# The seam between two convolution layers: where the second silu tile lies, how long a scratch tile is, and when the last store is issued

## Chip, core and metric

The kernel runs on one core of a Trainium2 chip. The metric is the device time of one execution in microseconds; lower is better. The core has five engines with queues of their own: TensorE (PE), VectorE (DVE), ScalarE (ACT), GpSimd (POOL) and SyncE (SP, which issues most of the transfers). Sixteen DMA engines carry out all transfers.

## The reference

The input x is 4 images of 16 channels, 256 by 256, float32. There are two residual layers:

```python
x = x + _L0_conv_ref(_gn(x), conv_w, conv_b)       # layer 0
x = x + _L1_conv_ref(_gn(x), base_weight, ...)     # layer 1
```

`_gn` is a group norm over 8 groups of two channels. Layer 0 makes 25 logits per channel and pixel with a 3x3 convolution, takes their softmax and weighs the pixel's 5x5 neighbourhood with it. Layer 1 is a 3x3 convolution of 16 to 16 channels on two kinds of features of the normed x: silu, and eight cubic B-spline bases. Its own group norm needs the sums of layer 0's result over a whole image.

## The kernel before

**Layer 0** works on 64 strips (4 images, 2 halves of the height, 8 strips of 32 columns). For each strip TensorE makes logits, ScalarE the exponentials `e`, GpSimd the products with the neighbourhood (L860), VectorE the sums (L700) into `nd`. The division follows in three VectorE instructions (L720 to L722), and GpSimd subtracts the result from `xc`, the block of x of four strips, so that `xc` holds layer 0's result x1 (L728). When a block is complete, `statistics` takes its sums and `store` writes it to `x1s` in HBM (L781). Both are put off by some steps with `after(k, f)`, which runs `f` k steps later. ScalarE's queue issues the stores; the last one only, of the last block of image 3, is issued by GpSimd. The last block also has a form of its own of the statistics, `last_statistics`: sixteen short VectorE instructions on `xc` (L759 and L763), and then eight of GpSimd on 128x8 elements (L766 to L773).

**Layer 1** works on 64 units (16 for each image), each of 16 rows. A unit n loads three things from `x1s` through SyncE's queue:

- `load_x` (L942): two halves of 1 MB into one of three tiles `xta`, `xtb`, `xtc` (unit n takes tile n % 3), each channel repeated on eight partitions;
- `load_tiles` (L957): four pieces of 128 KB into the upper 64 partitions of one of three silu tiles `sl[n % 3]`;
- and later `store` (L1026) writes the two pieces of output.

`silu` (L972, ScalarE) makes the silu features in the lower 64 partitions of the same tile. `features` makes the splines in two halves: ScalarE takes the distances to the grid in place (L990), `minus_r` is VectorE's share (L158), and `spline` goes through ScalarE (L163 to L166) and VectorE (L167 to L169) with scratch tiles `ta` for the first half and `tb` for the second, into `ring`. TensorE multiplies `ring` (L1036) and the silu tile (L1046) by the weights. `sides` (L1071) clears the two border columns of a silu tile with GpSimd.

The order within each engine is written out: `in_order` ties the instructions of each engine one behind the other as they are in the program, and `marks` and `behind` let the beginning of layer 1 move between the last instructions of layer 0. Thus units 0 and 1 are loaded while layer 0 is ending.

The tiles of layer 1 lie in the memory that layer 0's tiles gave back. They are placed one behind the other in the order in which the pools are opened, and a tile that covers an address of an older tile waits for everything that still uses the older one:

```python
xt0, tmp0, tmp1 = fixed("xta", XT), temps("ta"), temps("tb")
xt1, pad = fixed("xtb", XT), fixed("pad", [P, W + 2])[0]
ring = fixed("ring", [P, 3 * RU + 2, W + 2])[0]
SL = [P, RU // RT, W + 2]
sl = fixed("sl", SL)
xtt = xt0 + xt1 + fixed("xtc", XT)
sl += fixed("slb", SL, 2)
```

So the order of places is xta, ta, tb, xtb, pad, ring, one silu tile, xtc, two silu tiles. The order of the first loads on SyncE's queue is x of unit 0, silu rows of unit 0, x of unit 1, then x of unit 2, silu rows of unit 1, x of unit 3, silu rows of unit 2 and so on.

Of the kernel before, what the change touches and what calls it, by code (L numbers as in the profile page):

```python
# [11 lines left out]
F32 = mybir.dt.float32  # L12
# [22 lines left out]
def conv_preact_kernel(  # L35
# [13 lines left out]
    B, C, H, W = x.shape  # L49
    G = 8  # L50
    GC = C // G
    P = 128
# [23 lines left out]
    RU = 16  # L76
# [47 lines left out]
    for r in range(RT):  # L124
        p = P // 2 + SROWS.index(r + 1) * C
# [278 lines left out]
    with tc.tile_pool(name="prep0", bufs=2) as prep, tc.tile_pool(  # L404
        name="pre", bufs=1
    ) as pre, tc.tile_pool(
        name="xin", bufs=3
    ) as xin, tc.tile_pool(name="stat", bufs=2) as stat, tc.tile_pool(
        name="pstat", bufs=1, space=PSUM
# [116 lines left out]
        for b in range(B):  # L526
            st = stat.tile([P, G, NH * (GC if b == 0 else 1), 6], F32, name=f"st0_{b}", tag=f"st0{min(b, 1)}")
            for hf in range(NH):
                n = b * NH + hf
                t = loaded.pop(0)  # L530
# [80 lines left out]
    def newest(engine):  # L611
        return [i for i in nc.cur_bb.bb.instructions if i.engine == engine][-1]
# [7 lines left out]
    def layer0(shift):  # L620

        arm = "g" if shift else ""
        marks = {}
        first = len(nc.cur_bb.bb.instructions)
        with tc.tile_pool(name=f"prep{arm}", bufs=2) as prep, tc.tile_pool(
            name=f"im{arm}", bufs=NIM
        ) as imp, tc.tile_pool(name=f"l0{arm}", bufs=2) as l0, tc.tile_pool(
            name=f"nd{arm}", bufs=3
        ) as ndp, tc.tile_pool(name=f"x1{arm}", bufs=3) as x1p, tc.tile_pool(name=f"ptr{arm}", bufs=1, space=PSUM) as ptr, tc.tile_pool(
            name=f"plog{arm}", bufs=3, space=PSUM  # L630
# [44 lines left out]
            def load_xc(n):  # L675
                b, hf, s = strips[n]
                xc = x1p.tile([P, C, CX], F32, name=f"xc_{n}{arm}", tag="xc")
                nc.sync.dma_start(
                    xc, x[b, :, hf * P : (hf + 1) * P, s * SW : s * SW + CX].rearrange(
                        "c p w -> p c w")  # L680
                )
                return xc
# [5 lines left out]
            def after(k, f, *args):  # L688

                later.append([k, partial(f, *args)])  # L690
# [34 lines left out]
            def apply(n, nd, xc):  # L725
                w0 = strips[n][2] * SW % CX
                v = xc[:, :, w0 : w0 + SW]
                nc.gpsimd.tensor_sub(v, v, nd[:, 1])  # L728
                seeds[1:] = [newest(POOLE)]
                if w0 + SW == CX:  # L730
                    if n == len(strips) - 1:
                        after(1, last_statistics, n, xc)
                    else:
                        for g in range(G):
                            after(1 + g, statistics, n, xc, g)
                    after(2, store, n, xc)

            def columns_of(n):
                b, hf, s = strips[n]
# [35 lines left out]
            def store(n, xc):  # L775
# [10 lines left out]
                    name=nc.get_next_instruction_name(), engine=mybir.EngineType.Activation,  # L786
# [8 lines left out]
            nxc, xc = load_xc(0), None  # L795
            ahead = iter(())
            for n, (b, hf, s) in enumerate(strips):
# [12 lines left out]
                if s * SW % CX == 0:  # L810
                    xc = nxc

                nd = ndp.tile([P, 2, C, SW], F32, name=f"nd_{n}{arm}", tag="nd")
                for j in range(0, SW, JG):
                    if j % CI == 0:
                        k = n * nci + j // CI
# [68 lines left out]
    def layer1(arm, last, marks, seeds):  # L885
# [5 lines left out]
        with ExitStack() as pools:  # L891
            def pool(name, bufs=1, **kw):
                return pools.enter_context(tc.tile_pool(name=f"{name}{arm}", bufs=bufs, **kw))


            def temps(name):
                p = pool(name)
                return [p.tile([P, RU // 2 + 1, W], F32, name=f"{name}{k}{arm}") for k in range(3)]

            def fixed(name, shape, n=1):  # L900
                p = pool(name)
                t = [p.tile(shape, F32, name=f"{name}{k}{arm}") for k in range(n)]
                return t

            XT = [P, RU + 1, W]
            xt0, tmp0, tmp1 = fixed("xta", XT), temps("ta"), temps("tb")
            xt1, pad = fixed("xtb", XT), fixed("pad", [P, W + 2])[0]
            ring = fixed("ring", [P, 3 * RU + 2, W + 2])[0]
            SL = [P, RU // RT, W + 2]
            sl = fixed("sl", SL)  # L910
            xtt = xt0 + xt1 + fixed("xtc", XT)
            sl += fixed("slb", SL, 2)
            yop = pool("yo", 3)
            pstat = pool("pstat1", space=PSUM)
            py = pool("py", 4, space=PSUM)
# [1 line left out]
            units = [(b, u) for b in range(B) for u in range(NU)]  # L917

            def rows(t, dims, r):

                return bass.AP(tensor=t.tensor, offset=t.offset + r * W, ap=dims)
# [4 lines left out]
            def halves(u):  # L926
                lo, hi = span(u)
                mid = (lo + hi + 1) // 2
                return lo, ((lo, mid), (mid, hi))
# [8 lines left out]
            def load_x(n, half):  # L938
                b, u = units[n]
                lo, hs = halves(u)  # L940
                a, z = hs[half]
                nc.sync.dma_start(  # L942
                    xtt[n % 3][:, a - lo : z - lo, :],
                    rows(x1s[b], [[CP, C], [0, NS], [1, (z - a) * W]], u * RU - 1 + a),
                )
# [3 lines left out]
            def load_tiles(n):  # L949
                b, u = units[n]  # L950
                t = sl[n % 3][P // 2 :, :, 1 : W + 1]
                for p, q in outside(u):
                    nc.gpsimd.memset(t[p : p + C, q], 0.0)  # L953
                for k, d in enumerate(SROWS):
                    q0 = 1 if (u, d) == (0, 0) else 0
                    q1 = RU // RT - (1 if (u, d) == (NU - 1, RD - 1) else 0)
                    nc.sync.dma_start(  # L957
                        t[k * C : (k + 1) * C, q0:q1, :],
                        rows(x1s[b], [[CP, C], [RT * W, q1 - q0], [1, W]], u * RU - 1 + d + q0 * RT),
                    )  # L960

            def outside(u):

                return [
                    (SROWS.index(d) * C, q)
                    for at, d, q in ((0, 0, 0), (NU - 1, RD - 1, RU // RT - 1)) if u == at
                ]

            def silu(n):
                b, u = units[n]  # L970
                t = sl[n % 3][0 : P // 2, :, 1 : W + 1]
                nc.scalar.activation(  # L972
                    t, sl[n % 3][P // 2 :, :, 1 : W + 1], AF.Silu,
                    scale=sc[b][0][P // 2 :], bias=sc[b][1][P // 2 :],
                )
                for p, q in outside(u):
                    nc.gpsimd.memset(t[p : p + C, q], 0.0)

            def features(n, between):
                b, u = units[n]  # L980
                lo, hs = halves(u)
                r0 = place(n)
                parts = [
                    (a, z, xtt[n % 3][:, a - lo : z - lo], [t[:, 0 : z - a, :] for t in tmp])
                    for (a, z), tmp in zip(hs, (tmp0, tmp1))
                ]

                def distance(a, z):
                    t = xtt[n % 3][:, a - lo : z - lo]
                    nc.scalar.activation(t, t, AF.Abs, scale=sc[b][2], bias=sc[b][3])  # L990


                if n > 0:
                    distance(lo, hs[1][1])
                    minus_r(parts[1][3][0], parts[1][2])
                for k, (a, z, xt, tmp) in enumerate(parts):
                    if n == 0:
                        distance(a, z)
                    if k == 1:
                        between()  # L1000
                    spline(ring[:, r0 + a : r0 + z, 1 : W + 1], xt, *tmp, given=n > 0 and k == 1)
# [20 lines left out]
            def store(lag=LAG1):  # L1022
                if len(waiting) >= lag:
                    b, u, yo = waiting.pop(0)
                    for g in range(2):
                        nc.sync.dma_start(  # L1026
                            rows(out[b], [[W, 8], [H * W, C], [1, W]], u * RU + 8 * g), yo[:, g]
                        )
# [31 lines left out]
            load_tiles(0)  # L1060
            for half in range(2):
                load_x(1, half)
            nc.gpsimd.tensor_copy(pad, edge[:, 4:5].to_broadcast([P, W + 2]))
            for e in (0, W + 1):
                nc.gpsimd.tensor_copy(
# [3 lines left out]
            def sides(t):  # L1069
                for e in (0, W + 1):  # L1070
                    nc.gpsimd.memset(t[:, :, e : e + 1], 0.0)  # L1071

            halo(0)
            set_up = newest(POOLE).name
            sides(sl[0])
            features(0, put)
            first_silu = len(nc.cur_bb.bb.instructions)
            silu(0)
            for n in range(len(units)):
                if n % 2:  # L1080
                    next(more, None)
                if n > 0:
                    features(n, put)
                    silu(n)
                    halo(n)
                if n + 2 < len(units):
                    for half in range(2):
                        load_x(n + 2, half)
                store()
                if n + 1 < len(units):  # L1090
                    load_tiles(n + 1)
                outputs(n)
                if n == 0:
                    for t in sl[1:]:
                        sides(t)
            for _ in range(LAG1):
                put(1)
                store(1)
# [15 lines left out]
    with tc.If(fast > 0) as small_logits:  # L1114
        layer1("", *layer0(False))
    with small_logits.Else():
        layer1("g", *layer0(True))
# [42 lines left out]
```

## Time and profile before

| | us |
|---|---|
| median of 3 runs | 3076.96 (3075.38 to 3077.81) |
| the profiled execution | 3072.98 |
| its span | 3070.8 |
| VectorE busy | 2959.4 (96%) |
| TensorE busy | 2807.1 (91%) |
| ScalarE busy | 2238.8 (73%) |
| GpSimd busy | 1954.8 (64%) |
| mean granted TensorE clock | 0.967 |

All durations come from the one profiled execution, whose span is 2.2 us shorter than its time. The two layers show in its busy shares over time: GpSimd is busy for nine tenths of layer 0 and for hardly any of layer 1, ScalarE is full in layer 1. Layer 0's last sums on VectorE end at about 2046 us; the stretch up to 2100 us is the seam. An engine's line in a timeline gives its start, its duration, the engine, the line of the kernel and the operation with the tiles that it writes and reads; brackets give the idle time before it and the instruction that ended it. "SPq" is SyncE issuing a transfer: its duration is that of the issue and not of the transfer.

### The profile page before, as it was taken

To read this page: it belongs to the slowest core of one execution; us is meant where nothing else is said; L and a number is where in the kernel's file an instruction comes from. 1 tells how busy PE (TensorE), PEld (TensorE's weight loads), DVE (VectorE), ACT (ScalarE), POOL (GpSimd) and SP (SyncE) were. 2 spreads that over 40 slices of the span, in tenths; PEclk is the share of its full clock that TensorE was granted. 3 is DMA by queue.
4 is the path that set the end of the run, shared out by engine and by line. 5 is a ranking of instruction groups with operands and counts; after the bars stand their busy time and mean duration, and the time that the engine had idled before them with its cause. 6 is when DMAs were issued, how large, how long until landed. Compare 5 with 4: busy or idle time off the path is not lost.

```text
span 3070.8 us, 39744 instructions
## 1 busy us (share of the span) xinstructions
PE 2807.1 (91%) x14248; PEld 1450.3 (47%) x14248; DVE 2959.4 (96%) x1587; ACT 2238.8 (73%) x2587; POOL 1954.8 (64%) x744
## 2 busy tenths in 40 slices
PE   4599999999999999999999999957999999999998
PEld 3366656656566656666666656531222222222222
DVE  7599999999999999999999999997999999999997
ACT  6466675576765666765645646667999999999996
POOL 4299999999999999999999999971100100000000
PEclk7699999999999999999999999978999999999999
DMA  8988977879888778878867657659999999999994
GB/s 272 297 222 224 247 218 197 232 184 256 225 218 233 201 206 238 234 209 226 224 162 189 184 149 199 175 118 179 193 193 196 199 195 188 198 197 201 189 199 90
DMA packets 350929, 626.29 MB, mean 204 GB/s; under 512 B 41330, under 2 KB 216676, under 8 KB 334852
## 3 DMA queue, kind: packets, MB, share of 16 engines
q1 hardware_dynamic: 318020, 605.29, 80.6%
q10 hardware_dynamic: 30960, 15.73, 1.8%
q0 software_dynamic: 1744, 2.64, 0.3%
q8 instruction: 117, 1.92, 0.3%
q14 instruction: 88, 0.72, 0.1%
HBM read 513.95 MB, written 104.24 MB: 201 GB/s over the span
## 4 chain that ended last, share of the span: by engine, by line
DVE 69%; issue 11%; PE 7%; DMA 6%; ACT 3%; POOL 2%; SPq 2%; DVEq 0%; ACTq 0%; POOLq 0%
DVE nd L700 44%; PE lg L832 4%; DVE ta L168 4%; DVE ta L167 4%; DVE tb L168 4%; DVE tb L167 4%; DVE tb L158 2%; POOL e L860 1%; DVE yo L1019 1%; DVE r L721 1%; PE lg L836 1%; DVE nd L720 1%; DMA xta<-x1s 1%; DVE nd L722 1%; DMA an<-hsl 1%
## 5 line engine op out<-in xcount | busy, mean ns | idle before, releaser
L860 POOL TENSOR_TENSOR e<-e,u 128x1600 f32<-128x1600 f32 x512 | 1789.4, 3552 | 48.4 <-ACT e L855 30.5
L832 PE MATMUL lg<-wm,am 128*128 128x400 f32 x4096 | 1737.1, 505 | 82.6 <-ACT e L855 47.3
L700 DVE TENSOR_REDUCE nd<-e 128x128 f32<-128x3200 f32 x512 | 1748.0, 3478 | 28.3 <-POOL e L860 28.1
L836 PE MATMUL lg<-wn,an 97*128 97x400 f32 x2048 | 1345.8, 657 | 15.3 <-DMA an<-hsl 15.2
L855 ACT ACTIVATE e<-lg 128x800 f32<-128x800 f32 x1024 | 820.5, 838 | 709.6 <-DVE nd L700 472.3
L832 PEld LDWEIGHTS lg<-wm,am 128*128 128x128 f32 x4096 | 761.8, 192 | 402.3 <-ACT e L855 96.4
L1036 PE MATMUL yp<-ring,wt 128*32 128x512 f32 x6144 | 748.7, 600 | 97.0 <-DVE ring L169 73.1
L836 PEld LDWEIGHTS lg<-wn,an 97*128 97x128 f32 x2048 | 388.3, 190 | 333.9 <-issue 23.1
L1036 PEld LDWEIGHTS yp<-ring,wt 128*32 128x32 f32 x6144 | 205.4, 109 | 632.3 <-issue 428.9
L953 POOL MEMSET sl<- 16x256 f32 x4 | 1.2, 306 | 307.6 <-PE yp L1046 301.4
L953 POOL MEMSET slb<- 16x256 f32 x4 | 1.2, 307 | 299.8 <-PE yp L1046 299.7
L168 DVE TENSOR_TENSOR ta<-ta,ta 128x2048 f32<-128x2048 f32 (+1 forms) x64 | 147.4, 2304 | 3.4 <-ACT ta L166 3.3
L169 DVE SCALAR_TENSOR_TENSOR ring<-ta,ta 128x2048 f32<-128x2048 f32 (+1 forms) x64 | 147.8, 2310 | 2.5
L747 ACT ACTIVATE z<-xc,nrm 128x256 f32<-128x256 f32 x240 | 144.2, 601 | 5.4 <-POOL xc L728 1.3
L169 DVE SCALAR_TENSOR_TENSOR ring<-tb,tb 128x2048 f32<-128x2048 f32 x64 | 145.6, 2275 | 2.5
L168 DVE TENSOR_TENSOR tb<-tb,tb 128x2048 f32<-128x2048 f32 x64 | 145.3, 2270 | 0.0
L1046 PE MATMUL yp<-slb,ws 64*32 64x512 f32 (+1 forms) x1008 | 128.2, 602 | 0.0
L166 ACT ACTIVATE ta<-ta 128x2048 f32<-128x2048 f32 (+1 forms) x64 | 123.4, 1928 | 2.0
L193 POOL TENSOR_TENSOR d<-d,nrz 128x8 f32<-128x8 f32 x4 | 2.7, 666 | 188.1 <-DVE d L191 188.1
L166 ACT ACTIVATE tb<-tb 128x2048 f32<-128x2048 f32 x64 | 120.5, 1883 | 0.0
L972 ACT ACTIVATE slb<-slb,q 64x2048 f32<-64x2048 f32 x42 | 87.9, 2094 | 21.5 <-DMA slb<-x1s 20.4
L728 POOL TENSOR_TENSOR xc<-xc,nd 128x512 f32<-128x512 f32 x64 | 83.3, 1302 | 8.3 <-DVE nd L722 8.3
(195 smaller groups left out, 2099.3 us busy)
## 6 DMA issues: line engine op xcount, KB each, us to landing
am<-hst SPq DMA_DIRECT2D x512, 194.6 KB
u<-hs SPq DMA_DIRECT2D x320, 288.0 KB
an<-hsl SPq DMA_DIRECT2D x512, 129.8 KB
xta<-x1s SPq DMA_DIRECT2D x40, 1024.0 KB
xtb<-x1s SPq DMA_DIRECT2D x40, 1024.0 KB
xtc<-x1s SPq DMA_DIRECT2D x40, 1024.0 KB
am<-hst SPq DMA_DIRECT2D x256, 129.8 KB
slb<-x1s SPq DMA_DIRECT2D x164, 128.0 KB
```

Of the source, the lines that this page charges most:

```text
L166: nc.scalar.activation(s1, r1, AF.Square, scale=2.0)
L167: nc.vector.scalar_tensor_tensor(s2, t, 2.0, s2, ALU.subtract, ALU.mult)
L168: nc.vector.tensor_mul(s1, s1, r1)
L169: nc.vector.scalar_tensor_tensor(f, s2, 0.0, s1, ALU.min, ALU.subtract if given else ALU.add)
L700: nc.vector.tensor_reduce(nd[:, :, :, j : j + JG].rearrange("p t c j -> p t j c"), e.rearrange("p t j m c d -> p t j c m d"), AX.XY, ALU.add,)
L747: nc.scalar.activation(z, v, f, scale=nrm[b][:, 0, g : g + 1], bias=nrm[b][:, 1, g : g + 1], accum_out=st1[b][:, t, g, columns_of(n) : col ...
L832: nc.tensor.matmul(lg[:, i, :NL], lhsT=am[:, o : o + P], rhs=wm.rearrange("p m c d -> p (m c d)"), start=True, stop=False,)
L836: nc.tensor.matmul(lg[:, i, :NL], lhsT=an[:, o : o + P], rhs=wn.rearrange("p m c d -> p (m c d)"), start=False, stop=True,)
L855: nc.scalar.activation(ev, lg[:, :, :NL], AF.Exp)
L860: nc.gpsimd.tensor_tensor(e[:, 1].rearrange("p j m c d -> p j (m c) d"), e[:, 0].rearrange("p j m c d -> p j (m c) d"), uv, ALU.mult,)
L1036: nc.tensor.matmul(yp[t * M : (t + 1) * M], lhsT=wt[:, d, e].rearrange("p r o -> p (r o)"), rhs=ring[:, r0 + t * RT + d : r0 + t * RT + d ...
L1046: nc.tensor.matmul(yp[t * M : (t + 1) * M], lhsT=ws[v, e].rearrange("p r o -> p (r o)"), rhs=sl[n % 3][v, t : t + NT + 1 : NT, e : e + W], ...
```

## The change

Three edits, all at the seam:

1. The second silu tile is placed beside the first, ahead of `xtc`; only the third stays behind `xtc`. Its rows (unit 1) are loaded directly behind the x of unit 1, ahead of the x of unit 2, and its borders are cleared together with those of the first.
2. The scratch tiles `tb` of the second half of a unit have 8 rows instead of 9.
3. The last store of x1 is issued directly behind the last subtraction, ahead of `last_statistics`; it was issued two steps after it, behind the statistics. All other stores stay where they were.

```diff
                 if w0 + SW == CX:
                     if n == len(strips) - 1:
+                        store(n, xc)
                         after(1, last_statistics, n, xc)
                     else:
                         for g in range(G):
                             after(1 + g, statistics, n, xc, g)
-                    after(2, store, n, xc)
+                        after(2, store, n, xc)
...
-            def temps(name):
+            def temps(name, rows):
                 p = pool(name)
-                return [p.tile([P, RU // 2 + 1, W], F32, name=f"{name}{k}{arm}") for k in range(3)]
+                return [p.tile([P, rows, W], F32, name=f"{name}{k}{arm}") for k in range(3)]
...
-            xt0, tmp0, tmp1 = fixed("xta", XT), temps("ta"), temps("tb")
+            xt0, tmp0, tmp1 = fixed("xta", XT), temps("ta", RU // 2 + 1), temps("tb", RU // 2)
...
-            sl = fixed("sl", SL)
+            sl = fixed("sl", SL, 2)
             xtt = xt0 + xt1 + fixed("xtc", XT)
-            sl += fixed("slb", SL, 2)
+            sl += fixed("slc", SL)
...
             for half in range(2):
                 load_x(1, half)
+            load_tiles(1)
...
             halo(0)
             set_up = newest(POOLE).name
-            sides(sl[0])
+            for t in sl[:2]:
+                sides(t)
...
                 store()
-                if n + 1 < len(units):
+                if 0 < n < len(units) - 1:
                     load_tiles(n + 1)
                 outputs(n)
                 if n == 0:
-                    for t in sl[1:]:
-                        sides(t)
+                    sides(sl[2])
```

In the profile before, the silu tiles are called `sl` (the first) and `slb` (the second and third); with the change they are `sl` (the first and second) and `slc` (the third).

## The prediction

> **What bounds the kernel now.** I read the two-stage balance first, then the seam between the stages. Over most of the span VectorE is the engine without pauses: the profile gives it 96%, and the chain of waits 69%. Only the seam can change here, so I read the timeline of each engine from 2046 to 2105 us. First VectorE: start, duration, operation, and in brackets the idle time before it and its releaser.
> ```profile
> 2079.96 2.29 DVE L169 SCALAR_TENSOR_TENSOR ring<-tb,tb 128x2048 f32<-128x2048 f32 x1
> 2098.99 1.23 DVE L158 TENSOR_SCALAR tb<-xtc 128x2048 f32<-128x2048 f32 x1 [16.74 <-ACT xtc L990]
> ```
> VectorE ends unit 1 at 2082.25 and stands still for 16.74 us. It waits for ScalarE's distances of unit 2 (L990), and ScalarE was itself held up one instruction earlier:
> ```profile
> 2072.56 1.91 ACT L166 ACTIVATE tb<-tb 128x2048 f32<-128x2048 f32 x1
> 2093.03 2.09 ACT L972 ACTIVATE slb<-slb,q 64x2048 f32<-64x2048 f32 x1 [18.57 <-DMA slb<-x1s]
> 2095.15 3.80 ACT L990 ACTIVATE xtc<-xtc,q 128x4096 f32<-128x4096 f32 x1
> ```
> The silu of unit 1 wants its rows. SyncE issues those at 2086.19, in its queue behind the load of xtc:
> ```profile
> 2063.87 1.16 SPq L942 DMA_DIRECT2D xtc<-x1s  x2
> 2086.19 1.73 SPq L957 DMA_DIRECT2D slb<-x1s  x4
> 2087.96 2.02 SPq L942 DMA_DIRECT2D xta<-x1s  x2
> ```
> SyncE's own waits give the reason: 21.1 us for `x1s<-xc`, the last store of layer 0, because slb lies where that store reads. GpSimd shows why the store is late:
> ```profile
> 2062.57 1.27 POOL L728 TENSOR_TENSOR xc<-xc,nd 128x512 f32<-128x512 f32 x1 [8.32 <-DVE nd L722]
> ...
> 2068.38 2.13 POOL L767 TENSOR_TENSOR sq<-sq,nrm 128x8 f32<-128x8 f32 x1
> 2070.47 0.20 POOL L768 TENSOR_TENSOR sq<-mv,nrm 128x8 f32<-128x8 f32 x1
> ...
> 2079.96 1.28 POOL L781 DMA_DIRECT2D x1s<-xc  x1
> 2086.19 0.22 POOL L1071 MEMSET slb<- 128x8 f32 x4 [4.95 <-DMA x1s<-xc]
> ```
> Its data is complete at 2063.84, but the eight small statistics (L766 to L773) stand ahead of it until 2080. So the path through the seam is: statistics, store, slb, silu, distances. The last question is what limits the time behind it. In the windows view (length, the engines' busy time, clock, DMA share, GB/s):
> ```profile
> 2060.50:2065.00 4.50, 3.05 (x16) 0.80 (x20) 3.25 (x7) 3.64 (x1) 1.51 (x2) 0.50 0.00 0
> 2065.00:2074.50 9.50, 9.50 (x82) 2.40 (x74) 9.02 (x17) 9.41 (x6) 7.05 (x6) 0.91 0.98 216
> 2076.50:2081.50 5.00, 2.27 (x14) 0.29 (x10) 4.96 (x3) 0.00 (x0) 4.65 (x3) 0.89 0.00 0
> 2087.00:2184.00 97.00, 78.82 (x642) 19.65 (x638) 82.47 (x46) 90.29 (x43) 5.78 (x4) 0.89 1.03 192
> ```
> Before 2087 the DMA engines have holes (shares of 0.00); from 2087 to 2184 they are full. At 2184 comes ScalarE's one later wait for data, 1.84 us for slb at 2186.38, and VectorE loses 1.45 us at 2198.03 from it. So for the first hundred microseconds of layer 1 the loads are as much the limit as VectorE.
>
> **What the Trainium skill says.** "DMA: Bandwidth & Descriptors", Issuing engines are not separate DMA queues: loads and stores of all issuers share the same 16 engines. The trace agrees: the share is 1.03 with all of them running. The same page, Queues, rings and completion order: on each engine a queue's descriptors are consumed in ring order. In half-microsecond windows slb's bytes run from 2087.0, end in a dip at 2091.2, and xta's follow until a dip at 2100.2; so 4.2 us for four slb pieces and 9.0 for two xt halves, one behind the other. "SBUF — State Buffer", Who interferes with whom: a two-input VectorE instruction blocks a GpSimd instruction that reads SBUF. The trace agrees: L767 takes 2.13 us beside two-input instructions and L768 0.20 us. That is what makes the statistics long.
>
> **The change part by part.** Times are those of the profiled execution.
>
> *Store behind the subtraction.* Nothing is added: the same DMA moves past L977 and L766 to L773. It follows L728 at about 2063.9. From issue to landing it took 6.2 us (DMA issues view), so it lands at 2070.1, 16 us earlier. Its 1.28 us of issue end at 2065.2; the statistics wait for VectorE until 2067.2 anyway, so they keep their times, and their first reader (scales of image 3) comes many units later. VectorE's bn_stats (L759) read the same xc while it is stored; two readers need no wait.
>
> *Second silu tile beside the first.* In the changed program's list of waits, the rows of unit 1 (now sl1) wait only for older loads, and stand directly behind xtb (2048.1). Issue ends by about 2053, since the third piece waits for the first piece of sl0, landed by 2052.5. In ring order their 4.2 us of bytes follow xtb's, which end at 2060.1, into the empty stretch 2060.5 to 2065. Two more memsets of 0.06 us stand ahead of L728, under its 8.32 us of waiting. Silu(1) then runs right behind L166, at 2074.5 to 2076.6 instead of 2093.03. Cost zero.
>
> *What is late next.* The list puts the store's wait at the load of xtc: it waits for the store, POOL, ACT, DVE. So it leaves at 2070.1 instead of 2063.87, 6.2 us later, and queued behind it on SyncE are xta of unit 3, slc of unit 2 and xtb of unit 4, none of which could go earlier than 2087 before. From xtc's issue to its first bytes 1.15 us (2063.87 to 2065.0), 9.5 us of bytes, and 1.25 us until ScalarE starts (xtb: 2060.1 to 2061.36): 11.9, so 2082.0. A thin tail of xtc's traffic until 2076.3 makes it 13.6 at most: 2083.7. L990 and the start of VectorE take 3.84: VectorE starts unit 2 at 2085.9 (to 2087.6) instead of 2098.99. **13.1 us earlier for the compute (11.4 with the tail).**
>
> *The shorter scratch.* The second half of a unit has at most eight rows, so no instruction changes its shape. It only makes room; cost zero, covered by nothing because there is nothing to cover.
>
> *What of it reaches the end.* The transfers start their full stretch with xta: at 2070.1 + 1.15 + 9.5 = 2080.8 instead of 2091.2, **10.4 us earlier**, less than the compute's 13.1. As they are full until 2184, silu(7) gets its rows about 10.4 us earlier, and ScalarE and VectorE wait 2 to 3 us spread over units 2 to 8. Some dips in the DMA share (2162 to 2163.5, where a ring copy waited for VectorE) should close: I take 0.5 us. Behind 2204 the share falls to 0.91 and the lead stays to the end; TensorE's unit (11.34 + 3.03 us in the chain's last unit) fits within VectorE's 15.25 (2116.59 to 2131.85). Sum: 10.4 + 0.5 = 10.9, so **11 us**. The profiled execution took 3072.98 (span 3070.8), which gives 3062; it lies 4.0 under the median of the runs, 3076.96, from which I get **3066**.
>
> **The rivals.** *The loads do not bind* (the dips close wholly, or ring order is loose): all 13.1 arrive, up to 14.5 where the 1.45 of 2198 goes too: 3063. For it: ScalarE lost only 1.84 us in before. Against: a share of 1.03 for 97 us.
> *A partial gain*: sl1's pieces mix with xtb's and with the store. Each of these could lose up to sl1's 4.2 us; a delayed store passes it on to the whole queue: 11 less 4.2, 3070.
> *The wait for POOL at xtc means the statistics* (end 2080.0) and not L728; the list names the engine only. Then xtc leaves at 2080.0, xta's bytes start at 2090.7, 0.5 earlier than before: 3076. Against: in before xtc's load also waited for POOL, and left 0.03 us after L728.
> *The store starves, slower.* GpSimd writes its descriptors itself; before, that fell just ahead of VectorE's pause, now it falls into 16 us without one. If it were blocked until VectorE stops at 2082.25, it would land 6.2 later, at 2088.4, xta's bytes start at 2099.1, 7.9 us later than before: 3085. It decides against the change when the store lands after 2080.5 (10.4 later than I expect). For it: the tenfold L767. Against: bn_stats at 2063.88 has one input, and the old issue ran beside a two-input L169 in 1.28 us.
>
> **How the numbers follow.** The main case, 9 to 12.5 us, 0.60; all of it, 0.17; partial, 0.09; statistics, 0.08; starving, 0.06. About 0.2%, 6.2 us, is what a measurement can tell from no change. Faster: 0.60 + 0.17 + 0.06 of the partial case = 0.83; same: 0.03 + 0.08 + 0.01 = 0.12; slower 0.05. The range 3062 to 3071 (15 to 6 us) holds the first two cases and most of the third, and the spread of the medians of 1 to 2 us; the last two, 0.14, stay outside.
>
> **What would show it.** Right: the store at 2063.9, silu(1) at about 2074.5 without a wait, xtc issued at 2070, VectorE's pause 3.5 to 5.5 us, and afterwards waits of ScalarE for silu rows (L972) of 2 to 3 us in sum. Wrong: xtc issued after 2075, xtb later than 2061.4, a store longer than 8 us, or ScalarE's waits for loads over 5 us in sum.

## The result, and the profile after

| | before | with the change |
|---|---|---|
| median of 5 runs, us | 3076.96 (3075.38 to 3083.41) | 3061.86 (3059.24 to 3065.84) |
| ratio to before, 95% interval | | 0.9948 (0.9927 to 0.997) |
| the profiled execution, us | 3072.98 | 3061.86 |
| its span, us | 3070.8 | 3059.8 |
| VectorE busy, us | 2959.4 (96%) | 2959.0 (97%) |

The change makes the kernel faster by 15.1 us between these medians, where 10.9 was forecast; 3061.86 lies just below the range of 3062 to 3071. VectorE's work is the same, so what went is waiting. I read the same views as before, in the same order. First VectorE's timeline, the end of unit 1 and the start of unit 2:

```profile
2073.14 2.32 DVE L168 TENSOR_TENSOR ta<-ta,ta 128x2048 f32<-128x2048 f32 x1 [1.39 <-ACT ta L166]
...
2082.23 2.29 DVE L169 SCALAR_TENSOR_TENSOR ring<-tb,tb 128x2048 f32<-128x2048 f32 x1
2089.64 1.23 DVE L158 TENSOR_SCALAR tb<-xtc 128x2048 f32<-128x2048 f32 x1 [5.12 <-ACT xtc L991]
```

The pause is 5.12 us instead of 16.74; it is still there. ScalarE's timeline shows that the wait has changed its object:

```profile
2074.83 1.89 ACT L166 ACTIVATE tb<-tb 128x2048 f32<-128x2048 f32 x1
2076.74 2.09 ACT L973 ACTIVATE sl<-sl,q 64x2048 f32<-64x2048 f32 x1
2085.80 3.81 ACT L991 ACTIVATE xtc<-xtc,q 128x4096 f32<-128x4096 f32 x1 [6.97 <-DMA xtc<-x1s]
```

The silu of unit 1 runs right behind L166, without the 18.57 us for its rows. What ScalarE now waits for is x of unit 2. SyncE's timeline tells when that was issued, and its list of waits (us in total, times, longest) what it waited for:

```profile
2050.55 2.15 SPq L958 DMA_DIRECT2D sl<-x1s  x4
2072.72 1.16 SPq L943 DMA_DIRECT2D xtc<-x1s  x2
2073.93 1.49 SPq L943 DMA_DIRECT2D xta<-x1s  x2
```
```profile
SPq L943 <- DMA x1s<-xc: 19.9, 1, 19.9
```

The wait for the last store has moved from the silu rows to the load of xtc. GpSimd's timeline shows the store itself:

```profile
2063.88 1.27 POOL L728 TENSOR_TENSOR xc<-xc,nd 128x512 f32<-128x512 f32 x1 [8.25 <-DVE nd L722]
2065.45 1.26 POOL L782 DMA_DIRECT2D x1s<-xc  x1 [0.30 <-POOL xc L728]
...
2069.69 2.13 POOL L768 TENSOR_TENSOR sq<-sq,nrm 128x8 f32<-128x8 f32 x1
2071.78 0.20 POOL L769 TENSOR_TENSOR sq<-mv,nrm 128x8 f32<-128x8 f32 x1
```

The store leaves right behind its subtraction. The statistics behind it are done by 2073.4, where the prediction left them at 2080: after L768 each takes 0.20 to 0.25 us. In this stretch VectorE stood still for 1.39 us (until 2073.14 in its timeline; before, the pause there was 0.45 us), so no two-input instruction was in GpSimd's way. That agrees with the Trainium skill, "SBUF — State Buffer", Who interferes with whom, which the prediction drew on.

**One origin for all kernels.** Layer 0 isn't touched, yet its length differs from execution to execution: its last L700 ended between 2041.17 and 2052.84 us in the profiles of this document. So I count from the end of its last L700 (2046.11 before, 2047.41 after) and call the time from there to the span's end the tail. Each number below is a start in a timeline less that origin; the first two columns are issues, the third the start of VectorE in unit 2.

| profiled execution | last store | x of unit 2 | unit 2 on VectorE | pause | tail |
|---|---|---|---|---|---|
| before | 33.85 | 17.76 | 52.88 | 16.74 | 1024.69 |
| changed | 18.04 | 25.31 | 42.23 | 5.12 | 1012.39 |
| changed, e1_again | 18.05 | 25.31 | 41.40 | 4.52 | 1028.37 |
| changed, g1_again | 18.05 | 25.32 | 41.74 | 4.68 | 1020.84 |

At unit 2 the change is worth 10.65 us in this profile (52.88 less 42.23), and 12.3 at the end: the stall of 1.45 us at 2198.03 went as well. Layer 0 was 1.3 us longer, which leaves the 11.0 between the spans. The last two rows are the same program again: as early at unit 2, but up to 16 us later at the end. So the tail of a single execution can't carry a difference of a few us, and the experiments had to explain its scatter.

### The profile page after: what moved, and what is told of

The parts are those of the page before. It is cut to its first block, busy times and chain, and to the rows that moved or that the text cites. A ratio compares the mean times of both kernels' runs of the same rounds, so it can differ in the third digit from the quotient of the medians.

```text
span 3059.8 us, 39743 instructions
## 1 busy us (share of the span) xinstructions
PE 2802.6 (92%) x14248; PEld 1448.2 (47%) x14248; DVE 2959.0 (97%) x1587; ACT 2236.6 (73%) x2587; POOL 1947.6 (64%) x744
## 4 chain that ended last, share of the span: by engine, by line
DVE 69%; issue 11%; PE 8%; DMA 3%; ACT 3%; POOL 2%; SPq 1%; DVEq 0%; ACTq 0%; POOLq 0%
DVE nd L700 44%; PE lg L833 6%; DVE ta L168 4%; DVE ta L167 4%; DVE tb L168 4%; DVE tb L167 4%; DVE tb L158 2%; PE lg L837 1%; DVE yo L1020 1%; POOL e L861 1%; DVE r L721 1%; DVE nd L720 1%; DVE lo L370 1%; DMA am<-hst 1%; DVE nd L722 1%
## 5 line engine op out<-in xcount | busy, mean ns | idle before, releaser
L700 DVE TENSOR_REDUCE nd<-e 128x128 f32<-128x3200 f32 x512 | 1748.0, 3478 | 29.0 <-POOL e L861 28.9
L1047 PE MATMUL yp<-sl,ws 64*32 64x512 f32 (+1 forms) x1032 | 131.3, 602 | 0.0
L166 ACT ACTIVATE ta<-ta 128x2048 f32<-128x2048 f32 (+1 forms) x64 | 123.4, 1928 | 2.0
L166 ACT ACTIVATE tb<-tb 128x2048 f32<-128x2048 f32 x64 | 120.6, 1884 | 0.0
L973 ACT ACTIVATE sl<-sl,q 64x2048 f32<-64x2048 f32 x43 | 90.0, 2094 | 1.1
L728 POOL TENSOR_TENSOR xc<-xc,nd 128x512 f32<-128x512 f32 x64 | 82.5, 1289 | 8.2 <-DVE nd L722 8.2
```

Source lines behind the costliest of these rows:

```text
L166: nc.scalar.activation(s1, r1, AF.Square, scale=2.0)
L700: nc.vector.tensor_reduce(nd[:, :, :, j : j + JG].rearrange("p t c j -> p t j c"), e.rearrange("p t j m c d -> p t j c m d"), AX.XY, ALU.add,)
L1047: nc.tensor.matmul(yp[t * M : (t + 1) * M], lhsT=ws[v, e].rearrange("p r o -> p (r o)"), rhs=sl[n % 3][v, t : t + NT + 1 : NT, e : e + W], ...
```

## The experiments

The experiments are three series of four kernels (e, f and g), each series on a chip of its own; each kernel is set against the runs of the kernel before on the same chip. Those stood at 3074.51 us (67 runs, 3066.07 to 3091.59) for the kernels e, 3074.78 (45 runs, 3068.04 to 3093.59) for f, and 3073.93 (19 runs, 3067.52 to 3081.27) for g.

### e1_again and g1_again: the changed kernel, unaltered

> The changed kernel once more, to size the gain itself. Theory A (the seam gives 12 us, the rest of the first 15.1 us between the medians was spread of the runs): a gain of 11 to 13 us, ratio about 0.996. Theory B (the gain is larger than the seam shows, the change also speeds layer 0 or a later stage): again 15 us or more, ratio 0.995 or lower, and the profile shows layer 0 ending earlier than in the kernel before.

> The changed kernel once more, on the same chip as the three others of this call, since two earlier series of it stood 2.2 us apart (3061.9 from 5 runs, 3064.1 from 22). Expected 3064 us, runs from 3059 to 3075, 10 to 11 us under the kernel before.

Measured: 3064.05 us (22 runs, 3058.96 to 3074.87), ratio 0.9968 (0.9958 to 0.9978), a gain of 10.5; and 3062.44 (6 runs, 3057.67 to 3069.79), 0.9958 (0.9945 to 0.997), a gain of 11.5. All 33 runs of the changed program together have a median of 3063.62, and the 131 runs of before in the three series one of 3074.68: **11.1 us**. That is theory A's 11 to 13, not theory B's 15 or more. Five runs a side, drawn at random from these, give differences between 4.7 and 18.4 us in 95% of the draws, so the 15.1 of the first comparison is within their scatter. ScalarE's list of waits in e1_again shows what may scatter:

```profile
ACT sl L973 <- DMA sl<-x1s: 15.4, 11, 2.9
```

Eleven waits for silu rows in this execution, 15.4 us; in the one shown above there was none behind unit 2. In VectorE's timeline of e1_again they come out as waits for ScalarE of up to this size (0.72 us stand ahead of this one, from the same wait of ScalarE, 2.63 us):

```profile
2186.57 2.29 DVE L168 TENSOR_TENSOR ta<-ta,ta 128x2048 f32<-128x2048 f32 x1 [1.45 <-ACT ta L166]
```

The windows view of the first 200 us from the origin, for before, changed, e1_again and g1_again in this order (the last two columns are the DMA share and GB/s):

```profile
2046.11:2246.11 200.00, 160.24 (x1256) 41.55 (x1260) 177.18 (x115) 167.76 (x82) 30.79 (x27) 0.87 0.95 183
```
```profile
2047.41:2247.41 200.00, 169.32 (x1344) 43.93 (x1348) 189.22 (x122) 180.10 (x87) 22.87 (x27) 0.91 0.96 195
```
```profile
2044.33:2244.33 200.00, 168.69 (x1324) 41.14 (x1324) 185.53 (x119) 174.21 (x84) 24.82 (x27) 0.91 1.00 191
```
```profile
2046.96:2246.96 200.00, 167.51 (x1324) 40.62 (x1324) 184.66 (x119) 173.38 (x84) 27.32 (x27) 0.91 0.99 189
```

The same program moved 39.0, 38.2 and 37.8 MB in its first 200 us, and the two that moved less show the **higher** DMA share. A full share is thus no rate: 2 to 3% of delivery lie between an execution in which layer 1's loads keep ahead and one in which they don't. Why it differs, no run here shows.

### f1_light_after and f2_light_before: fewer bytes behind the seam

The same edit in both kernels; from unit 3 on three of four silu pieces are not loaded, so that the features of their rows come from older rows:

```diff
-                for k, d in enumerate(SROWS):
+                for k, d in enumerate(SROWS if n < 3 else SROWS[:1]):
```

> The changed kernel, from unit 3 of layer 1 on with one of the four pieces of each silu block loaded instead of four, so the features of the other rows come from older rows. Nothing at the seam is touched. Theory L (in many executions layer 1's loads bind, which spreads the runs from 3059 to 3075 us and takes part of the shift): without these bytes 3058 to 3060 us, all runs within about 4 us, no wait of ScalarE for silu rows, span from the end of layer 0's last blend some 1012 us. Rival S (the spread comes from elsewhere, layer 0 or the chip as a whole): median and spread as the changed kernel's own, 3064 and some 15 us.

> The same cut in the kernel before. Theory L: the pure compute shift remains between this one and the changed kernel with the cut, 10.7 us at unit 2's start and at most 12.3 to the end, so 3069 to 3072 us, and a narrow spread. Rival S: 3074.5 us with the spread of the kernel before (3066 to 3092).

Measured: 3060.59 us (8 runs, 3056.51 to 3062.72), ratio 0.994 (0.9921 to 0.996); and 3070.14 (22 runs, 3066.65 to 3075.03), 0.9982 (0.9972 to 0.9992). The spread of before falls from 25.5 us to 8.4, and of the changed kernel from the 15.9 of e1_again to 6.2 (in fewer runs), where 4 was expected. The standard deviations, which don't depend on the number of runs in this way, fall from 5.6 to 2.1 and from 4.5 (all 33 runs) to 2.0. So most of the spread, and 4.6 us of the median of before, came from these loads, as theory L has it. The cut takes transfers with their bytes; which of the two counts isn't shown. Between the two kernels with fewer bytes lie 9.55 us (the difference of the medians, 7.8 to 11.2 when their runs are drawn again), and 10.2 between their tails (1023.72 and 1013.53). ScalarE's waits of f2 keep the one of the seam, 18.8 us for slb; it is only the later ones that the cut takes:

```profile
ACT slb L972 <- DMA slb<-x1s: 18.8, 1, 18.8
```

This is what the change is worth where the loads don't bind. It is no more than where they do (11.1 over all runs), so the load stream did not eat the gain: both kernels lose to it, before 4.6 us of its median and the changed one 3.0 (3063.62 less 3060.59, of different series).

### e2_store_only: the early store without the layout

The kernel before with `store(n, xc)` moved, and nothing else:

```diff
                     if n == len(strips) - 1:
+                        store(n, xc)
                         after(1, last_statistics, n, xc)
...
-                    after(2, store, n, xc)
+                        after(2, store, n, xc)
```

> The kernel before with the early store alone; places of the tiles and order of the loads as before. Theory A (the store's landing was the only lock of the seam, and the other edits only shift which load waits for it): xtc is issued at about 2064 as before, slb 14 us earlier at about 2071.5, silu(1) at about 2084.5 instead of 2093, VectorE starts unit 2 at about 2090.3 instead of 2099: 9 to 10 us faster than before, nearly all of the change. Theory C (the parts only work together): under 3 us.

Measured: 3069.24 us (22 runs), ratio 0.998 (0.9969 to 0.9992), 5.3 us under before, between theory A's 9 to 10 and theory C's under 3. The DMA issues view (KB, us from issue to landing) and VectorE's timeline:

```profile
x1s<-xc POOLq DMA_DIRECT2D x1, 1024.0 KB, 14.6
```
```profile
2090.35 1.23 DVE L158 TENSOR_SCALAR tb<-xtc 128x2048 f32<-128x2048 f32 x1 [8.95 <-ACT xtc L991]
```

In this order of loads xtc's two megabytes leave 0.3 us before the store, and beside them it took 14.6 us instead of 6.2. The silu rows, which wait for it, were issued at 32.7 from the origin; unit 2 started at 44.98, 7.9 us earlier than before. Little of it reached the end in this execution: the tail is 1023.53, 1.2 under before's, and seven more waits of ScalarE for slb followed, 8.1 us in sum:

```profile
ACT slb L973 <- DMA slb<-x1s: 18.9, 8, 10.8
```

The Trainium skill, "DMA: Bandwidth & Descriptors", SWDGE vs HWDGE vs iDMA, says that GpSimd's and the other issuers' transfers feed different queues between which each DMA engine takes turns. The trace agrees that they share, which before's share of 1.03 with SyncE's transfers alone could not show; that the store would land only at the end of all that moved (3.2 MB from 2064.4 to 2078.1, by the windows view) is not in the page.

### e3_layout_only: the layout without the early store

The changed kernel with that diff taken back.

> The changed kernel with the store late again, behind the statistics: only the places, the shorter scratch and the order of the loads are changed. Theory A: xtc now has to wait for the store, which lands at about 2087, so that VectorE starts unit 2 at about 2104, 5 us later than before: 5 to 6 us slower than the kernel before. Theory C (the early silu tile is what frees the seam): 3 to 6 us faster.

Measured: 3074.64 us (14 runs), ratio 1.0001 (0.9986 to 1.0015): no difference, and not the loss that I expected. GpSimd's timeline and VectorE's:

```profile
2075.71 1.28 POOL L781 DMA_DIRECT2D x1s<-xc  x1
```
```profile
2098.40 1.23 DVE L158 TENSOR_SCALAR tb<-xtc 128x2048 f32<-128x2048 f32 x1 [13.67 <-ACT xtc L990]
```

I had left the store where it was in before, 33.85 from the origin; it came at 27.84. The statistics ahead of it were 6 us shorter, as in the changed kernel, since VectorE waited 1.12 us for ScalarE among them (until 2073.34). So x of unit 2 went out at 34.14, and unit 2 began at 50.53, 2.3 us earlier than before. Neither part makes the whole: 5.3 and 0 us alone, 10.5 together in the same series. The layout takes the silu rows out of the store's shadow but puts xtc there, and only the early store makes that shadow short.

### e4_long_scratch: the scratch tiles at nine rows

The changed kernel with `tb` at nine rows again; the second silu tile keeps its place behind the first and gets a pool of its own, and its borders are cleared as late as in the kernel before:

```diff
-            xt0, tmp0, tmp1 = fixed("xta", XT), temps("ta", RU // 2 + 1), temps("tb", RU // 2)
+            xt0, tmp0, tmp1 = fixed("xta", XT), temps("ta", RU // 2 + 1), temps("tb", RU // 2 + 1)
...
-            sl = fixed("sl", SL, 2)
+            sl = fixed("sl", SL) + fixed("slm", SL)
```

> The changed kernel with nine rows in the scratch of the second half again. The second silu tile then reaches 1.2 KB into a buffer that the last subtraction reads, so its rows wait for that subtraction (about 2065) and its borders are cleared after the store. Theory A: its bytes fall beside the store's, which lands 0 to 4 us later, and xtc with it: 0 to 4 us slower than the changed kernel, still 8 to 12 us faster than before. Theory D (the shorter scratch has a worth of its own in every unit): as slow as before or slower.

Measured: 3064.97 us (22 runs), ratio 0.9974 (0.9963 to 0.9984), 0.9 over e1_again, which the intervals don't tell apart. In its profile the silu rows of unit 1 left at 17.77 from the origin instead of 3.1. At 17.77 L728 releases `nd`: with the longer scratch the tile reaches into nd's place. Unit 2 started at 42.72 on VectorE, 0.5 to 1.3 us later than in the changed kernel's three profiles (its pause was 6.41 us). So the shorter scratch is worth about 1 us at the seam, which the runs can't resolve.

### f3_xtc_clear, g2_xtc_clear: xtc out of the last store's way

The remaining pause is xtc waiting for the store. Here xtc is placed over the two older x1 blocks and the sums' tile, and each block has a pool of its own, so xtc's place is free long before the store:

```diff
-        ... tc.tile_pool(name=f"x1{arm}", bufs=3) as x1p ...
+        ... tc.tile_pool(name=f"x1a{arm}", bufs=1) as x1a, ... as x1b, ... as x1c, ... as zp ...
...
-                xc = x1p.tile([P, C, CX], F32, name=f"xc_{n}{arm}", tag="xc")
+                xc = (x1a, x1b, x1c)[n // (CX // SW) % 3].tile([P, C, CX], F32, name=f"xc_{n}{arm}", tag="xc")
...
-                z = x1p.tile([P, GC * CX], F32, name=f"z_{n}_{g}{arm}", tag="z", bufs=1)
+                z = zp.tile([P, GC * CX], F32, name=f"z_{n}_{g}{arm}", tag="z", bufs=1)
...
-            xtt = xt0 + xt1 + fixed("xtc", XT)
             sl += fixed("slc", SL)
...
+            fixed("gap", [P, 436 * 4 + 240])
+            xtt = xt0 + xt1 + fixed("xtc", XT)
```

> The changed kernel with the tile of the passage x block xtc put over two older x1 blocks and the sums' tile, each x1 block with a region of its own, so that xtc's load no longer waits for the last store's region to be read. Its two loads go out right behind silu's, near 17.8 us after the end of layer 0's last blend instead of 25.3. Theory C (the pause of VectorE is what sets the end, the rest follows one for one): the pause of 5.1 us goes to 0 to 1, unit 2 starts at 37 to 39 instead of 41.4 to 42.2, and the time is 4 to 6 us under the changed kernel's. Theory L (the loads bind further on): 2 us or less, since the bytes are the same and only 7 us earlier; ScalarE waits for silu rows instead. The store then runs beside xtc's bytes, and may take some 15 us instead of 7; nothing but the tile of the next load waits for it.

> The kernel with xtc over the two older x1 blocks, again, beside the changed kernel. Its first series of 6 runs stood at 3053.9 us, which is 10 us under the changed kernel, while its profiled execution accounts for 7.2: the pause of 5.1, 0.4 and some 1.6 of three short waits of VectorE. Theory W (the waits at the seam are the whole of it): 7 us under the changed kernel in this call. Rival D (the order of loads, xtc ahead of the store, also spares later waits for silu rows): 9 to 11 us under it, and a smaller spread of its runs than 15 us.

Measured: 3053.85 us (6 runs, 3051.63 to 3061.46), ratio 0.9926 (0.9899 to 0.9953); and 3056.46 (6 runs, 3053.87 to 3062.79), 0.9945 (0.9931 to 0.9958), 6.0 us under g1_again (0.0 to 11.3 when the runs are drawn again), which holds theory W's 7 and rival D's 9 to 11. **This version beats both**: over its 12 runs the median is 3055.7, 8.0 under the changed kernel's 33 (2.5 to 10.7) and 19.0 under before. Theory C's 4 to 6 lies in that interval, theory L's 2 just outside. VectorE's and SyncE's timelines of f3:

```profile
2080.14 2.29 DVE L169 SCALAR_TENSOR_TENSOR ring<-tb,tb 128x2048 f32<-128x2048 f32 x1
2082.35 1.22 DVE L158 TENSOR_SCALAR tb<-xtc 128x2048 f32<-128x2048 f32 x1
```
```profile
2051.13 1.16 SPq L944 DMA_DIRECT2D xtc<-x1s  x2
2056.34 5.70 SPq L944 DMA_DIRECT2D xta<-x1s  x2
```

The pause is gone: unit 2 starts at 36.58 from the origin, 5.65 us before the changed kernel's. xtc leaves at 5.36, earlier than the 17.8 I expected. The tail is 1005.13, 7.3 under the changed kernel's: pause 5.12, and two waits of VectorE that shrank (from 0.72 and 1.46 to 0.57 together, and from 1.39 to 0.95). The store did take 18.2 us beside these loads, but unit 2 didn't wait for it; what did was SyncE's first transfer of output, for 3.6 us.

### g3_xtc_clear_light

The version above with the cut of f1.

> The same with one of the four pieces of each silu block from unit 3 on instead of four, so the features of the other rows come from older rows. Theory W: 7 us under the changed kernel with that cut (3060.6), 3053 to 3054, and 3 to 4 under the uncut one. Rival D: 3053 to 3054 too, but within 1 us of the uncut one.

Measured: 3053.60 us (5 runs), ratio 0.9934 (0.9921 to 0.9947): 7.0 under f1_light_after, though of another series; theory W expected 7. Against the uncut one, g2, it is 2.9 lower, with an interval that holds both theories (2.0 higher to 8.6 lower when the runs are drawn again). What speaks for W is g2's profile: four waits of ScalarE for silu rows again, of 0.33 to 1.46 us. The runs leave W and D open. On the spread, 11.2 us over the 12 uncut runs, so few runs decide nothing.

### f4_extra_load, g4_extra_load2: more bytes

The changed kernel with rows that nobody reads loaded behind xtc in unit 0: four pieces (0.5 MB) in f4, eight (1 MB) in g4.

```diff
+            dummy = fixed("dummy", [P, RU // RT, W])[0]
...
+                    if n == 0:
+                        for k in range(4):
+                            nc.sync.dma_start(
+                                dummy[P // 2 + k * C : P // 2 + (k + 1) * C],
+                                rows(x1s[0], [[CP, C], [RT * W, RU // RT], [1, W]], RU - 1 + k),
+                            )
```

> The changed kernel with 0.5 MB of rows that nobody reads loaded into a spare tile between xtc's and xta's loads. Rival slack (loads have room in most executions): 0 to 1 us over the changed kernel. Theory L (the stream of layer 1's loads binds for the first 300 us): 0.5 MB at some 190 to 205 GB/s is 2.5 us, up to 4.2 us if these rows into 16 partitions are as slow as silu's; so 2.5 to 4.2 us more, seen as later silu rows at ScalarE.

> The changed kernel with 1 MB of rows that nobody reads loaded between xtc's and xta's loads (0.5 MB stood at 3066.3 in the call before, 2.3 over the changed kernel of another call, with both intervals overlapping). Rival slack: at most 1 us over the changed kernel of this call. Theory L: 5 to 8 us over it, seen as waits of ScalarE for slc, xta or later silu rows.

Measured: 3066.34 us (22 runs), ratio 0.9971 (0.996 to 0.9982), 2.3 over e1_again, which is of another series; and 3067.84 (14 runs), 0.998 (0.9969 to 0.9991), 5.4 over g1_again. The first doesn't decide, the second is what theory L expected, though the interval of the difference (0 to 8.9, drawn likewise) touches the rival's. The tails don't decide it: 1015.66 and 1017.76 lie within the changed kernel's own three (1012.39 to 1028.37). The waits at units 2 and 3 are clearer. ScalarE's and VectorE's timelines of g4:

```profile
2104.95 2.09 ACT L974 ACTIVATE slc<-slc,q 64x2048 f32<-64x2048 f32 x1 [5.94 <-DMA slc<-x1s]
```
```profile
2110.90 1.23 DVE L158 TENSOR_SCALAR tb<-xta 128x2048 f32<-128x2048 f32 x1 [3.46 <-ACT xta L992]
```

Directly behind the seam the loads have little slack: 1 MB more there is 5.94 us of waiting for slc (2.43 for 0.5 MB), where the changed kernel's three profiles had 0.50 at most. VectorE began unit 3 at 62.86 from the origin, 3.0 to 3.8 us later than in those three (59.02 to 59.86). With 0.5 MB unit 3 began 17.65 behind unit 2, as in the changed kernel (17.63), so VectorE lost nothing by those 2.43.

## Why the prediction was right in size and its range missed

**The mechanism at the seam held.** The store left 18.04 from the origin (17.8 forecast); silu(1) ran at 29.33 without a wait (28.4 forecast); xtc took over the wait for the store; GpSimd issued the store in 1.26 us without a stop, and it landed by 2072.72, so the starving rival fell. The rival that xtc waits for the statistics fell too, though not by the 2080 that it named, as they ended at 2073.4. In g1_again xtc left 5.1 us before their end:

```profile
2075.10 2.28 POOL L774 TENSOR_SCALAR st<-sq 128x8 f32<-128x8 f32 x1
```
```profile
2072.28 1.16 SPq L943 DMA_DIRECT2D xtc<-x1s  x2
```

**The compute's 13.1 us was 10.65.** Unit 2 was forecast at 39.8 from the origin and came at 42.23. Three terms were short: the store left 0.2 later; xtc left 7.3 us behind the store's issue instead of 6.2; and from xtc's issue to L991 it was 13.08 us instead of 11.9, within the 13.6 that the prediction allowed for a tail. In the last 11.8 of these, 2.6 MB moved (221 GB/s in the windows view), half a megabyte more than xtc's two; part of that fell into the 1.25 us until ScalarE starts, the rest ran beside xtc's. So ring order was looser than the 9.5 us for xtc alone assumed, and the profile before had shown it: from 2087.0 to 2091.2 the windows view has 157 GB/s, that is 0.66 MB, where slb's four pieces are 0.52. Together 2.5. The pause is 5.12 instead of 3.6 and not 6.0, because xtb came later as well, and VectorE ended unit 1 one us later. ScalarE's timelines before and with the change:

```profile
2061.36 3.80 ACT L990 ACTIVATE xtb<-xtb,q 128x4096 f32<-128x4096 f32 x1 [5.45 <-DMA xtb<-x1s]
```
```profile
2063.61 3.81 ACT L991 ACTIVATE xtb<-xtb,q 128x4096 f32<-128x4096 f32 x1 [6.21 <-DMA xtb<-x1s]
```

That is 15.25 and 16.20 from the origin. The rows of unit 1, now issued directly behind xtb, were put at no cost; ScalarE started on xtb at 15.8 to 16.6 in the profiles of all kernels that load them there, and at 15.1 to 15.4 where they come later (before, e2, e4 and f2). This is a small part of the partial-gain rival.

**The loads' 10.4 us was the wrong limit in this execution, and near the right number.** I made the load stream the bound and took the lesser of the two shifts. In the profiled execution ScalarE never waited for silu rows behind unit 2, so the compute's 10.65 reached the end, with 1.65 on top. In e1_again and g1_again it did wait, 18 and 9 us in sum, over the 5 that the prediction named as a sign of being wrong; xtb later than forecast was another such sign. Whether the loads bind is not a property of the program alone: the bytes delivered in 200 us differed by 3%. I had read the share of 1.03 as a fixed rate. That 10.9 met the 11.1 of all runs is thus in part luck: a compute shift put too high was cut by a limit that doesn't bind in every execution.

**The step that failed** is the last one, "it lies 4.0 under the median of the runs, 3076.96, from which I get 3066". That offset came from three runs. Over 131 runs the median is 3074.68, and the profiled execution lies 1.7 under it; 3062 plus 1.7 is 3063.7, where the 33 runs of the changed program stand (3063.62). The gain of 10.9 was right (11.1). Likewise the range took "the spread of the medians of 1 to 2 us": the medians of one program, in different series, were 3076.96, 3074.51, 3074.78 and 3073.93 for before, 3061.86, 3064.05 and 3062.44 for the change, 3.0 and 2.2 apart. Of the 4.1 us between 3066 and 3061.86, 2.3 are the offset (4.0 where 1.7 holds over all runs) and 1.8 the five runs of the changed kernel, whose median lies that far under that of the 33. A difference of two medians of five runs can be off by 7 us, and the low end of the range was 4 under the forecast.

## What to carry to other kernels

Where a load waits for memory and not for data, ask what else lies in that memory. Taking one tile out of a late store's shadow moves the wait to the next tile in it; the gain comes when the shadow is short, and the rest when nothing that is needed soon lies in it. Where two engines and the load stream are all nearly full, take the time from as many runs as can be had, and compare profiles from a common event behind the untouched part rather than by their spans.

## What the runs showed of the hardware that I had not expected

- The same program delivered 189 to 195 GB/s over the same 200 us at DMA shares of 0.96 to 1.00; the execution with the lowest share was the fastest.
- A store of 1 MB from GpSimd took 6.2 us from issue to landing alone, 7.1 a little behind other bytes, 14.6 beside 2 MB of loads and 18.2 in a longer stream of them. In f3 both together moved 320 GB/s from 2070.80 to 2080.80, against some 220 for xtc's loads alone in the changed kernel; in the 7 us before, with silu rows among the loads, they moved 211.
- The silu rows' four pieces went at 113 GB/s at a share of 1.05 (2062.50 to 2065.50 in the changed kernel), half the rate of xtc's at 1.01.
